# Transformer block with depthwise convolution: one band fewer on TensorE in the last image, and other offsets for the instruction order

## The chip, the cores and the metric

The kernel runs on one core of one Trainium2 chip. The core has five engines with instruction streams of their own: TensorE (PE; its weight loads are shown as PEld), VectorE (DVE), ScalarE (ACT), GpSimd (POOL) and SyncE (SP), and 16 DMA engines that they share. The metric is the device time of one execution in microseconds (us), as the median of several executions.

## What is computed

The input x is 16 images of 128 channels by 96 x 96 pixels, in fp32. For each image:

```python
x_hwc = x.transpose(0, 2, 3, 1)
xn1 = layernorm(x_hwc)                       # over the 128 channels
q, k, v = xn1 @ wq.T, xn1 @ wk.T, xn1 @ wv.T # 8 heads of 16 channels, q and k L2-normed over the pixels
attn = softmax(q @ k.T * 16 ** -0.5)         # 16 x 16 per head: channels against channels
x = x + (attn @ v) @ wp.T
xn2 = layernorm(x)
h1 = w_in @ xn2                              # 1x1 convolution, 128 -> 512 channels
h2 = depthwise_3x3(h1, w_dw)                 # 9 taps per channel, padding 1
x = x + w_out @ gelu(h2)                     # 1x1 convolution, 512 -> 128
```

## The kernel before

**Tiling.** An image is 8 bands of 12 rows; a band is 3 units of 4 rows (384 pixels). The 512 hidden channels are 4 chunks of 128. Over all images there are 128 bands, and a pair of band and chunk that goes through the vector path is a "job".

**Stages of an image.** The first norm (`norm`, line 555, with `second` false) loads x, transposes it on PE (line 614, tile pT_a), takes statistics on DVE (621), a variance and a power on POOL (628, 632), scales on ACT (668), sums the Gram matrix on PE (682) and transposes back (719). `attention` (757) makes one 128 x 128 matrix per image from the Gram matrix. The second norm begins with `x2` (564): PE multiplies the normed pixels by that matrix (571, "mix"), ACT evicts the result into one of six x buffers (580, "mixed"), and an accumulating DMA issued from POOL adds the original x to it (583, "add_x"). The transposes that follow (614, pT_b, "forth_b") read the sum; statistics, scaling and the transposes back (719, "back_b") give the padded input of the convolution.

**The feed-forward part of a band.** There are two ways for a chunk.

- The vector path, `conv_job` (886). PE makes the hidden rows (906, "hidden"), ACT copies them into a padded tile (911, "kept"). ACT multiplies two of the nine taps (919, "products"; three taps for chunk 1). The sum of these is made by accumulating DMAs issued from POOL (940), and a last one of them adds that sum to the band's tile h3. The centre tap is scaled to one, and the six (five) others are multiply-adds on DVE: the first one (924) writes h3, the rest (930) update it. ACT applies gelu (944). If the next band takes the same path, ACT first copies the last two hidden rows to the head of the padded tile (902, "halo"), and the next band makes only 12 new rows.
- By matmuls, `by_matmuls` (976), for chunk 3 alone. The 1x1 convolution and a tap are one matrix for each tap, so the nine taps are nine products per unit that add up in PSUM (990, "conv"), 27 for a band, and ACT applies gelu from PSUM (1000).

`by_pe` (1040) says which bands send chunk 3 to PE: 7 in every 15, and for the last image those that `PE_LAST` lists, counted from the end (0 is band 7, 7 is band 0). Before, these are bands 7, 6, 4, 3 and 1. With them there are 451 jobs. After the four chunks, `ffn_out` (1008) multiplies by w_out on PE (1017), DVE adds x (1024), and SP stores the band (1028), in the last band unit by unit.

**What sets the order.** Every engine runs its instructions in the order of the program, and that order is made when the program is built. Each piece of work is entered with `op` (73): its engine, an assumed duration, a place, what it reads and writes. The place is counted in jobs: the job's number plus an offset from the table `AT` that belongs to the kind of work. `Plan.order` (103) then plays the whole program through: whenever an engine is idle, it takes the piece with the lowest place among those whose inputs are done and whose buffers are free. Some buffers (`IN_TURN`, line 36) are handed out strictly by place. The starting times of this play give the program's order. The kinds whose name ends in `_0` hold for the first image.

```python
def at(kind, place, i=1):
    return place + AT[kind if i else kind + "_0"]
...
def by_pe(g):
    k = NG - 1 - g
    return k in PE_LAST if k < NB else k % PE_OF in PE_BANDS
```

Of the kernel before, what the change touches and what calls it, by code (L numbers as in the profile page):

```python
# [19 lines left out]
PE_CHUNK = 3  # L20
PE_BANDS = (0, 2, 4, 6, 8, 10, 12)
PE_OF = 15
PE_LAST = (0, 1, 3, 4, 6)
TINY = 1e-20
UNIT_MIN = 1e-18
UNIT = 4
# [8 lines left out]
X1_BUFS, XB_BUFS, PR_BUFS, H3_BUFS, ZT_BUFS = 2, 6, 5, 10, 3  # L35
IN_TURN = ("tr", "h3", "pr", "xb", "x1")
AT = dict(
    load_w=-20.2, weights=13.4, zeros=-68.05, load_a=-147.85, forth_a=-13.65, stats_a=-60.15, variance_a=574.05,
    power_a=353.05, scaled_a=35.3, gram=0.3, back_a=-44.8, place_a=177.6, attention=-146.15, mix=-16.25,
    residual=204, mixed=-47.8, add_x=-331.2, forth_b=-11.5, stats_b=-104.75, variance_b=68.55, power_b=-326.9,  # L40
    shift_b=-87.05, scaled_b=162.15, back_b=-5.95, place_b=38.15, halo=227.9, hidden=2.75, kept=-114.4,
    products=153.15, add_last=-10.05, tap=4.7, add_first=-147.85, gelu=241.95, conv=3.5, conv_gelu=5.8, out=7,
    add=-70.85, store=278.2, mix_0=-75.3, residual_0=369.55, mixed_0=-142.3, add_x_0=-398.7, gram_0=126.2,
    forth_a_0=-269.2, forth_b_0=-14.9, stats_a_0=-113.85, stats_b_0=-48.05, scaled_a_0=100.95, scaled_b_0=286.6,
    back_a_0=-115.65, back_b_0=-181.55, place_a_0=-352.8, place_b_0=-9.75, shift_b_0=-101.75, late=-3.55,
)
STEP = dict(scaled=0.3, hidden=0.1, products=0.5, tap=0.166, conv=1.6, conv_tap=0.03, out=0.8, out_part=0.05)
SLACK = 300
# [164 lines left out]
def tile_restormer_block(  # L213
# [826 lines left out]
# [4 lines that stand above are left out]
# [58 lines left out]
```

## Time and profile before

| | us |
|---|---|
| median of 3 runs | 4140.04 |
| lowest and highest of them | 4127.82, 4140.15 |
| the profiled execution, its own time | 4139.28 |
| its span, first to last instruction | 4137.5 |

| engine | busy, us | of the span |
|---|---|---|
| PE | 4064.3 | 98% |
| DVE | 4048.7 | 98% |
| ACT | 3674.7 | 89% |
| POOL | 2538.1 | 61% |

The profile is of one execution. A group of instructions is named by its line, engine and operation, with the tile written and those read: `L930 DVE ... h<-h,ratio,h` is the multiply-add at line 930. An fp32 product appears as two records of PE, so line 990 has 3,294 records for 61 bands of 27 products. PE's records overlap, since matmuls are pipelined; what one costs is read from the starts of neighbours, not from its length. `<-` after an idle time names what ended it. Granted clock is the share of its full clock that TensorE was given.

### The profile page before, as it was taken

The numbers are of one execution on the slowest core, as the hardware profiler recorded it, in microseconds if no ns is written. First come the engines' busy times: TensorE is split into PE (matmuls) and PEld (weight loads), VectorE is DVE, ScalarE is ACT, GpSimd is POOL, SyncE is SP. The second block draws the span as 40 slices with busy tenths as digits, with TensorE's granted clock in tenths as the row PEclk, the third lists the DMA queues.
The fourth block names the chain that finished last, engine by engine and source line by source line (L and its number), as shares of the span: only waits on it lengthen the run. The fifth ranks groups of instructions, "written<-read, shape, count | busy, mean of one in ns | idle before, by whom it ended". The sixth has DMA issues, their size and how long they took to land.

```text
span 4137.5 us, 52025 instructions
## 1 busy us (share of the span) xinstructions
PE 4064.3 (98%) x17217; PEld 2630.9 (64%) x17217; DVE 4048.7 (98%) x4706; ACT 3674.7 (89%) x6993; POOL 2538.1 (61%) x2357
## 2 busy tenths in 40 slices
PE   8999999999999999999999999999999999999999
PEld 6666666666666666666666666666666666666555
DVE  6999999999999999999999999999999999999998
ACT  5899989999889998999899989999889989999886
POOL 4657656566665757657566665666646666566442
PEclk9999999999999999999999999999999999999999
DMA  2999999999999999999999999999999999999998
GB/s 87 193 195 213 205 213 204 206 217 199 211 203 204 209 198 209 216 200 207 199 216 197 209 201 206 213 207 204 200 198 211 205 213 209 194 208 205 192 195 187
DMA packets 205372, 833.50 MB, mean 201 GB/s; under 512 B 23728, under 2 KB 25136, under 8 KB 205104
## 3 DMA queue, kind: packets, MB, share of 16 engines
q0 software_dynamic: 165600, 678.37, 84.6%
q1 hardware_dynamic: 38256, 151.73, 9.8%
q8 instruction: 136, 2.23, 0.2%
q14 instruction: 132, 1.08, 0.1%
q10 hardware_dynamic: 1248, 0.09, 0.0%
HBM read 148.26 MB, written 75.50 MB: 54 GB/s over the span
## 4 chain that ended last, share of the span: by engine, by line
PE 40%; DVE 10%; ACT 5%; DMA 3%; issue 2%; POOL 1%; POOLq 0%; ACTq 0%; DVEq 0%
PE h L990 11%; PE h L1017 10%; PE h L906 8%; DVE h L930 7%; PE g L682 2%; PE h L571 2%; DMA h<-pr 2%; DVE h L924 2%; PE pB_a L719 1%; ACT pr L919 1%; PE pT_b L614 1%; PE pT_a L614 1%; PE pB_b L719 1%; DMA pr<-pr 1%; ACT h L911 1%
## 5 line engine op out<-in xcount | busy, mean ns | idle before, releaser
L930 DVE SCALAR_TENSOR_TENSOR h<-h,ratio,h 128x1140 f32<-128x1140 f32 (+3 forms) x2129 | 2890.9, 1378 | 5.0
L919 ACT ACTIVATE pr<-h,ratio 128x1152 f32<-128x1152 f32 x1028 | 1337.2, 1307 | 98.7 <-DMA h<-pr 63.1
L990 PE MATMUL h<-xn,comp 128*128 128x380 f32 (+1 forms) x3294 | 1160.5, 483 | 3.6 <-ACT h L911 1.5
L1017 PE MATMUL h<-h,woutT 128*128 128x384 f32 x3072 | 1129.9, 487 | 11.4 <-ACT h L944 4.7
L906 PE MATMUL h<-xn,winT 128*128 128x384 f32 (+2 forms) x2706 | 1055.9, 494 | 8.0 <-ACT h L911 6.1
L940 POOL DMA_DIRECT2D pr<-pr x578 | 558.3, 977 | 478.3 <-ACT pr L919 312.0
L990 PEld LDWEIGHTS h<-xn,comp 128*128 128x128 f32 x3294 | 596.9, 190 | 348.8 <-issue 6.5
L911 ACT COPY h<-h 128x384 f32<-128x384 f32 (+2 forms) x1353 | 670.0, 525 | 142.0 <-PE h L906 110.8
L1017 PEld LDWEIGHTS h<-h,woutT 128*128 128x128 f32 x3072 | 555.7, 190 | 347.1 <-issue 25.0
L906 PEld LDWEIGHTS h<-xn,winT 128*128 128x128 f32 x2706 | 485.6, 190 | 302.4 <-issue 35.9
L940 POOL DMA_DIRECT2D h<-pr x450 | 447.6, 998 | 361.5 <-PE h L906 73.8
L924 DVE SCALAR_TENSOR_TENSOR h<-h,ratio 128x1152 f32<-128x1152 f32 x451 | 633.8, 1408 | 5.0 <-ACT h L911 2.8
L944 ACT ACTIVATE h<-h 128x1152 f32<-128x1152 f32 x453 | 549.4, 1216 | 14.9 <-DMA h<-pr 8.9
L632 POOL TENSOR_TENSOR rstd_a<-ve_a,mhalf 128x4 f32<-128x4 f32 x288 | 535.3, 1859 | 13.0 <-POOL ve_a L628 0.2
L628 POOL TENSOR_SCALAR ve_a<-st_a 128x4 f32<-128x4 f32 x288 | 347.3, 1206 | 286.9 <-DVE st_a L621 263.2
L632 POOL TENSOR_TENSOR rstd_b<-ve_b,mhalf 128x4 f32<-128x4 f32 x288 | 516.5, 1794 | 10.6
L672 ACT ACTIVATE zT<-pT_b,nb_b,rstd_b 128x128 f32<-128x128 f32 x1132 | 434.3, 494 | 47.4 <-DVE nb_b L636 40.6
L628 POOL TENSOR_SCALAR ve_b<-st_b 128x4 f32<-128x4 f32 x288 | 285.5, 996 | 301.9 <-DVE st_b L621 285.5
L668 ACT ACTIVATE zT<-pT_a,rstd_a 128x128 f32<-128x128 f32 x1080 | 320.3, 422 | 18.9 <-POOL rstd_a L632 17.7
L682 PEld LDWEIGHTS g<-zT 128*128 128x128 f32 x2304 | 295.1, 192 | 45.0 <-issue 4.4
L682 PE MATMUL g<-zT 128*128 128x129 f32 x2304 | 305.1, 275 | 0.0
L571 PE MATMUL h<-xn,mwT 128*128 128x384 f32 x768 | 287.1, 490 | 6.6 <-ACT h L911 3.2
(171 smaller groups left out, 3585.7 us busy)
## 6 DMA issues: line engine op xcount, KB each, us to landing
pr<-pr POOLq DMA_DIRECT2D x578, 576.0 KB, 7.5
h<-pr POOLq DMA_DIRECT2D x450, 576.0 KB, 7.7
x<-in_x_dram SPq DMA_DIRECT2D x128, 576.0 KB, 6.8
out_dram<-x SPq DMA_DIRECT2D x127, 576.0 KB, 6.3
x<-in_x_dram POOLq DMA_DIRECT2D x122, 576.0 KB, 7.2
out_dram<-x SPq DMA_DIRECT2D x3, 192.0 KB, 1.9
weights<-in_L_conv_w_in_dram SPq DMA_DIRECT2D x1, 256.0 KB, 2.9
weights<-in_L_conv_w_out_dram SPq DMA_DIRECT2D x1, 256.0 KB, 3.0
```

The lines of the kernel that those rows point to most:

```text
L628: nc.gpsimd.tensor_scalar(ve, d["mv"][:, :, 2], 1.0 / C, EPS, ALU.mult, ALU.add)
L632: nc.gpsimd.tensor_tensor(rstd, d["ve"], mhalf, ALU.pow)
L682: nc.tensor.matmul(grams[i][:, : P + 1], lhsT=zt[:, :P], rhs=zt, start=(q == 0 and k == 0), stop=(q == NU * TPU // QT - 1 and k == QT - 1),)
L906: nc.tensor.matmul(rows(ph), lhsT=winT[:, n, :], rhs=window(xn, r0 + r, e - r, 1), start=True, stop=True)
L911: nc.scalar.copy(window(h1_, r, e - r, 1), rows(d.pop(("ph", r))))
L919: nc.scalar.activation(to, shifted(t), AF.Copy, scale=ratio[:, n, t : t + 1])
L924: nc.vector.scalar_tensor_tensor(h3, shifted(t), ratio[:, n, t : t + 1], shifted(UNIT), ALU.mult, ALU.add)
L930: nc.vector.scalar_tensor_tensor(to, shifted(t)[:, lo:hi, cut], ratio[:, n, t : t + 1], to, ALU.mult, ALU.add)
L940: nc.gpsimd.dma_start(out=to, in_=d["pr", t], accum_op=ALU.add)
L944: nc.scalar.activation(h3, h3, AF.Gelu)
L990: nc.tensor.matmul(d["pc"][:, lo:hi, cut], lhsT=comp[:, t, :], rhs=window(xn, r0 + dy, UR, dx)[:, lo:hi, cut], start=(t == order[0]), stop ...
L1017: nc.tensor.matmul(rows(d["po"]), lhsT=woutT[:, n, :], rhs=h3s[g, n][:, s * UR : (s + 1) * UR, :], start=(k == 0), stop=(k == NCH - 1),)
```

## The change

`PE_LAST` loses its 4: band 3 of the last image sends chunk 3 through the vector path, and PE does chunk 3 of bands 7, 6, 4 and 1. There are 452 jobs. Nearly all offsets of `AT` get other values. No function, buffer count, assumed duration or step changes.

```diff
-PE_LAST = (0, 1, 3, 4, 6)
+PE_LAST = (0, 1, 3, 6)
...
 AT = dict(
-    load_w=-20.2, weights=13.4, zeros=-68.05, load_a=-147.85, forth_a=-13.65, stats_a=-60.15, variance_a=574.05,
-    power_a=353.05, scaled_a=35.3, gram=0.3, back_a=-44.8, place_a=177.6, attention=-146.15, mix=-16.25,
-    residual=204, mixed=-47.8, add_x=-331.2, forth_b=-11.5, stats_b=-104.75, variance_b=68.55, power_b=-326.9,
-    shift_b=-87.05, scaled_b=162.15, back_b=-5.95, place_b=38.15, halo=227.9, hidden=2.75, kept=-114.4,
-    products=153.15, add_last=-10.05, tap=4.7, add_first=-147.85, gelu=241.95, conv=3.5, conv_gelu=5.8, out=7,
-    add=-70.85, store=278.2, mix_0=-75.3, residual_0=369.55, mixed_0=-142.3, add_x_0=-398.7, gram_0=126.2,
-    forth_a_0=-269.2, forth_b_0=-14.9, stats_a_0=-113.85, stats_b_0=-48.05, scaled_a_0=100.95, scaled_b_0=286.6,
-    back_a_0=-115.65, back_b_0=-181.55, place_a_0=-352.8, place_b_0=-9.75, shift_b_0=-101.75, late=-3.55,
+    load_w=-11.35, weights=26.85, zeros=-51.2, load_a=-148.1, forth_a=-12.95, stats_a=-77.6, variance_a=582.8,
+    power_a=359.6, scaled_a=34.95, gram=0.2, back_a=-48.25, place_a=192.25, attention=-147.25, mix=-9.95,
+    residual=188.1, mixed=-47.25, add_x=-337.85, forth_b=-10.25, stats_b=-123.85, variance_b=75.75,
+    power_b=-321.2, shift_b=-86.15, scaled_b=152.35, back_b=-1.25, place_b=26, halo=237.2, hidden=2.75,
+    kept=-122.9, products=147.25, add_last=-6.5, tap=3.55, add_first=-152.4, gelu=244.25, conv=3.35,
+    conv_gelu=4.1, out=7.05, add=-83.45, store=276.95, mix_0=-81.9, residual_0=376.05, mixed_0=-142.1,
+    add_x_0=-392.4, gram_0=138.4, forth_a_0=-265.5, forth_b_0=-14.9, stats_a_0=-103.3, stats_b_0=-56.85,
+    scaled_a_0=98.55, scaled_b_0=286.35, back_a_0=-116.6, back_b_0=-170.2, place_a_0=-343.35, place_b_0=-8.15,
+    shift_b_0=-113.75, late=10.8,
 )
```

## The prediction

> **What bounds the kernel now.** I read the page's busy table first, then the chain that ended last, then the busy time by stage, and last the timeline of the final 20 us, engine by engine.
>
> The busy table and the chain of the page:
> ```profile
> span 4137.5 us, 52025 instructions
> ...
> PE 4064.3 (98%) x17217; PEld 2630.9 (64%) x17217; DVE 4048.7 (98%) x4706; ACT 3674.7 (89%) x6993; POOL 2538.1 (61%) x2357
> ...
> PE 40%; DVE 10%; ACT 5%; DMA 3%; issue 2%; POOL 1%; POOLq 0%; ACTq 0%; DVEq 0%
> ```
> PE and DVE are both within 2.2% of the span, so neither can take work without the other giving some up. Work moved from one to the other helps only if the receiver has idle time where the work lands. That is read by stage; columns are the stretch, its length, then busy us (instructions) of PE, PEld, DVE, ACT, POOL, then granted clock, DMA share and GB/s:
> ```profile
> 0.00:100.00 100.00, 84.68 (x542) 69.12 (x543) 67.89 (x198) 50.73 (x133) 40.81 (x101) 0.98 0.28 86
> 100.00:1000.00 900.00, 885.34 (x3791) 574.63 (x3790) 889.83 (x1020) 818.57 (x1570) 580.06 (x520) 1.00 0.97 205
> 1000.00:2000.00 1000.00, 989.13 (x4234) 641.69 (x4233) 989.71 (x1138) 909.31 (x1749) 648.60 (x578) 1.00 0.97 206
> 2000.00:3000.00 1000.00, 985.85 (x4186) 640.04 (x4185) 983.77 (x1125) 907.86 (x1731) 636.97 (x571) 0.99 0.97 205
> 3000.00:3800.00 800.00, 791.61 (x3365) 511.58 (x3364) 791.41 (x911) 727.61 (x1389) 507.07 (x455) 1.00 0.97 206
> 3800.00:4100.00 300.00, 293.75 (x999) 174.02 (x998) 298.93 (x293) 249.17 (x413) 120.15 (x129) 0.99 0.96 198
> ```
> DVE's idle time is 32.1 us in the first 100 us, 10.2 + 10.3 + 16.2 + 8.6 = 45.3 us from 100 to 3800, and only 1.1 us from 3800 to 4100. That last stretch is the last image, where no next image's first norm runs beside the bands. PE is idle 6.2 us there. So in the very stage that the change touches DVE is full and PE almost.
>
> The end, from the timeline (start, length, engine, line, operation, count, idle before and its releaser):
> ```profile
> 4118.28 15.64 PE L1017 MATMUL h<-h,woutT 128*128 128x384 f32 x48
> ...
> 4123.47 1.30 DVE L930 SCALAR_TENSOR_TENSOR h<-h,ratio,h 128x1045 f32<-128x1045 f32 x1
> ...
> 4124.80 2.40 ACT L944 ACTIVATE h<-h 128x384 f32<-128x384 f32 x4 [5.84 <-DVE h L930]
> ...
> 4133.96 0.56 DVE L1024 TENSOR_TENSOR x<-h,x 128x384 f32<-128x384 f32 x1 [2.02 <-PE h L1017]
> ```
> DVE's last tap ends at 4124.8, the last gelu at 4127.2, but PE still has 24 output products queued and ends at 4133.9. The chain view of the last part agrees: it lies on DVE taps from about 3797 to 4076 and on PE from 4076.7 to 4133.9, without a gap. So DVE sets the pace of the last image and PE sets its last 57 us.
>
> **The change, part 1: band 3 of the last image.** In PE_LAST the number counts from the end, so the 4 that goes is band 3. Its channel chunk 3 goes from 27 tap matmuls to the vector path (line 976 on is no longer called for it, line 886 on is).
>
> PE: an fp32 product is two records. In the timeline, 22 conv records (L990) that begin at 4084.32 are followed by the next group at 4091.37: 0.320 us each. 27 x 2 x 0.320 = 17.3 us go. Three hidden products (L906; four rows each, since band 2 hands on a halo) come: 6 x 0.323 (15.49 us over 48 in the chain's last piece) = 1.9 us. Net PE -15.4 us.
>
> DVE: six taps come, one L924 and five L930. Start to start in the last 80 us an L924 takes 1.33 us (4061.92 to 4063.25) and four L930 5.28 (4065.03 to 4070.31), so 1.33 + 5 x 1.32 = +7.9 us. The page's means (1408 and 1378 ns) hold some overlap of one instruction's end with the next one's start.
>
> ACT, by the rows of the last image: 3 x 0.504 (kept) + 2 x 1.289 (products) + 1.157 (gelu of a band) + 0.403 (band 2 now copies a halo for chunk 3) - 3 x 0.509 (gelu of a unit) = +4.1 us. ACT has 51 us idle from 3800 to 4100, so this is hidden; without that cover it would cost its 4.1.
>
> POOL issues two more accumulating DMAs, 2 x 0.93 us, in a stretch where it is busy 40%: hidden. On the queue itself: 84.6% of 4137.5 us over 1,150 transfers (578 + 450 + 122) is 3.04 us of all 16 engines each, so +6.1 us. The DMA share from 3800 to 4100 is 0.96, some 12 us free. They fit, closely. SP's stores keep their number and order.
>
> **Sum of part 1.** DVE is full, so its 7.9 us come later at the end: last tap 4124.8 + 7.9 = 4132.7. What must follow a last tap, with no PE queue in the way: 2.4 us of gelu slices, one product pair 0.65, semaphores about 0.3 (an estimate from the 0.1 to 0.3 between such steps above), the add 0.56, and the 3.0 us between that add's end (4134.5) and the span's end, for the store: 6.9 us. That gives 4139.6, **+2 us**, if the 15.4 us taken off PE empty its queue at the end. If they do not, because bands 6 and 7 are still done by PE at the very end and their buffers come free only with DVE's progress, the whole PE block slides by DVE's delay: **+8 us**. PE idles only 6.2 us in the 300 before, so its block at the end is mostly backlog and most of it should be drawn forward: I take **+4**. A gain from part 1 alone is excluded: DVE's sum grows where it has 1 us idle.
>
> One page speaks against freeing PE at all. The Trainium skill, Perfetto Trace Analysis, section Identifying the Most-Contended Engine, says that TensorE's nearness to its limit is to be read from MFU and the busy share of weight loads, not from matmul busy time; here that share is 64% of the span, and 58% from 3800 to 4100, which would make PE's relief worthless and the sum +8. The row at 4118.28, 48 records at 0.32 us with no gap, says that PE was the one waited for, and I go by the row.
>
> **Part 2: the new order.** Nearly every offset in AT changes. An offset only chooses among operations whose inputs and buffers are ready, and the work and its durations stay. Moves of a whole band or more (3.5 jobs; a job is 4137.5 / 451 = 9.2 us): mix from -16.25 to -9.95 and back_b from -5.95 to -1.25 in PE's order, place_b 38.15 to 26 in ACT's, add_last -10.05 to -6.5 on POOL, late and weights 14 jobs later at the start. No row shows the new order, so I bound it by what one and the same order shows in different stretches. DVE's idle rate from 100 to 3800 runs from 10.3 per 1000 us to 16.2. Over 3700 us the best rate gives 38 us idle, -7; the worst 60, +15. Further out: all 45.3 us of stalls gone is -45, stalls doubled +45; the first 100 us hold another 32 that the start's offsets reach. The rows lie on both sides, so I take 0 and keep both ends.
>
> Total: +4 on the profiled execution's 4139.28 (its span is 4137.5; the other 1.8 lie around it). That execution is 0.8 under the median of the three runs, 4140.04, which is nothing beside their spread of 12.3. **4143.**
>
> **Rivals.**
> *The order loses more than it did (slower).* mix is put 6.3 jobs later while forth_b, which needs its result, moves by 1.25. Between them stand the ACT eviction and POOL's accumulating load, which lands 7.2 us after issue in the median, 13.3 at worst; x buffers, six, already hold mix back, which speaks against. Today only 5 of the 122 loads keep PE's weight loads waiting, 2.5 us in all. PE runs its list in order, so behind a late forth_b stand hidden products, convs and outputs, then DVE's taps. It decides once a band loses more than 0.07 us in the mean (8.4 us over 120 bands, with the +4 past the bound below). At the worst stretch's rate it is +19 (4158), with stalls doubled +49; middle 4165.
> *The last image's DMA fills up (slower).* 6.1 us more on a queue with 12 free, where taps wait for no transfer but the gelu does. If none of the free time can be used: 7.9 + 6.1 = +14, 4153. Against it: ACT's waits on accumulating transfers in the last 337 us are 13 us in all.
> *The order gains (faster).* Half of the 45.3 us of stalls goes: -23 + 4 = -19, 4120. For it: in several 100 us stretches (300 to 400, 2300 to 2400) DVE has no idle at all, so the stalls are not inherent. Against: PE is idle 48 us in the same 3700, both would have to lose theirs together.
>
> **Chances.** What a measurement of this kernel tells from no change is about 0.3%, 12.4 us: below 4127.6 faster, above 4152.5 slower. Forecast, within it: 0.34. Order loses 0.32, DMA 0.06: slower 0.38. Order gains: 0.28. The likeliest is the forecast, 4143, with its own range 4130 to 4152. Both signs hold most of the chance between them, so the 8 in 10 reach from the gain's price, 4120, to a little past the loss's middle, 4168.
>
> **What would show it.** L990 3240 records (54 fewer), L930 2134, L924 452, L940 two more. Right: DVE idle under 3 us from 3800 to 4100, its last tap some 8 us nearer to the span's end, so fewer than 48 output records after it, PE idle in the last image up by about 15, DVE idle from 100 to 3800 between 38 and 60. Wrong: waits of pT_b on x grown from 2.5 us (first rival), gelu waiting for transfers in the last image (second), DVE idle from 100 to 3800 under 30 (third), or a first 100 us with other than about 32 idle on DVE.

## The result, and the profile after

| | before | after |
|---|---|---|
| median of 22 executions each, us | 4136.72 | 4148.07 |
| lowest and highest | 4127.82, 4144.29 | 4135.63, 4162.76 |
| the profiled execution (its span) | 4139.28 (4137.5) | 4144.05 (4142.3) |

The ratio is 1.0029, with a 95% interval of 1.0020 to 1.0038: the changed kernel is slower by 11.4 us (8 to 16), just inside the 0.3% (12.4 us) that the prediction called no change, with an interval that reaches beyond it. The two profiled executions are 4.8 us apart, and not 11.4, because the one before lies 2.6 us above its median and the one after 4.0 us below. What the two traces show has to be read with that in mind. Line numbers of the changed kernel are one higher than before from line 46 on (`AT` has one line more): 931 is the tap that was 930.

The busy table of the page after:
```profile
span 4142.3 us, 51899 instructions
...
PE 4049.7 (98%) x17169; PEld 2623.6 (63%) x17169; DVE 4056.4 (98%) x4712; ACT 3682.2 (89%) x6997; POOL 2535.3 (61%) x2359
...
L931 DVE SCALAR_TENSOR_TENSOR h<-h,ratio,h 128x1140 f32<-128x1140 f32 (+3 forms) x2134 | 2905.6, 1383 | 5.1
```
Against before, PE has lost 14.6 us of busy time and DVE has gained 7.7: the move of the work came out as counted (2,134 and 452 taps, 3,240 conv records, two more transfers).

The same stretches as before, with the same columns:
```profile
0.00:100.00 100.00, 84.71 (x531) 69.23 (x532) 67.58 (x196) 50.27 (x130) 41.53 (x102) 0.95 0.27 86
100.00:1000.00 900.00, 883.91 (x3807) 575.34 (x3807) 891.50 (x1028) 818.26 (x1577) 571.35 (x519) 1.00 0.96 204
1000.00:2000.00 1000.00, 987.67 (x4207) 639.61 (x4205) 984.58 (x1121) 908.82 (x1736) 663.84 (x575) 1.00 0.97 206
2000.00:3000.00 1000.00, 988.21 (x4207) 642.05 (x4207) 990.00 (x1132) 910.57 (x1733) 631.36 (x572) 1.00 0.97 207
3000.00:3800.00 800.00, 792.15 (x3381) 514.39 (x3379) 792.38 (x917) 732.47 (x1400) 497.48 (x458) 1.00 0.97 206
3800.00:4100.00 300.00, 275.05 (x925) 161.02 (x925) 297.86 (x293) 246.12 (x407) 123.66 (x128) 0.98 0.94 195
```
DVE's idle time from 100 to 3800 is 8.5 + 15.4 + 10.0 + 7.6 = 41.5 us (45.3 before): no sign of a worse order in this execution. From 3800 to 4100 DVE idles 2.1 us (1.1) and PE 25.0 (6.2). The freed PE time lies idle in the last image.

The end, rows of the timeline:
```profile
4131.36 2.65 DVE L931 SCALAR_TENSOR_TENSOR h<-h,ratio,h 128x1056 f32<-128x1056 f32 x2
4133.19 2.40 ACT L945 ACTIVATE h<-h 128x1152 f32<-128x1152 f32 x4 [10.23 <-DMA h<-pr]
4134.41 4.14 PE L1018 MATMUL h<-h,woutT 128*128 128x384 f32 x12 [0.36 <-ACT h L945]
...
4138.59 0.56 DVE L1025 TENSOR_TENSOR x<-h,x 128x384 f32<-128x384 f32 x1 [0.73 <-PE h L1018]
```
The last tap ends at 4134.0, 9.2 us later than before. After it PE has 12 records left, not a queue of many bands, and the span ends 8.3 us later (12.7 before).

**A mark that splits the span.** The last image can be cut off at DVE's last residual add of image 14. The busy time from that mark to the end of the last tap, and from there to the end of the span (the tail); before:
```profile
3935.70:4124.80 189.10, 187.15 (x620) 110.36 (x620) 188.68 (x176) 142.67 (x229) 66.67 (x71) 1.00 0.94 197
4124.80:4137.50 12.70, 9.12 (x29) 5.06 (x27) 2.67 (x5) 2.40 (x4) 0.00 (x0) 0.96 0.24 93
```
and after:
```profile
3931.00:4134.00 203.00, 182.13 (x586) 105.63 (x584) 198.48 (x183) 145.93 (x232) 70.16 (x73) 0.97 0.91 192
4134.00:4142.30 8.30, 4.19 (x13) 2.20 (x12) 1.69 (x4) 1.60 (x4) 0.00 (x0) 1.00 0.19 71
```
From the mark on, 201.8 us became 211.3: +9.5. DVE's busy time up to the last tap grew by 9.8 (7.9 of taps; 0.9 are two residual adds that now come ahead of the last tap; the rest is a tap at the mark), its idle time by 4.1 (0.4 to 4.5), and the tail shrank by 4.4. The longest of DVE's waits there is one that the trace before does not have. By the view of waits (us in total, times, longest):
```profile
DVE h L925 <- PE h L1018: 3.1, 1, 3.1
```

### The profile page after: what moved, and what is told of

Read it like the earlier page. It is cut to its first block, busy times and chain, and to the rows that moved or that the text cites. A ratio compares the mean times of both kernels' runs of the same rounds, so it can differ in the third digit from the quotient of the medians.

```text
span 4142.3 us, 51899 instructions
## 1 busy us (share of the span) xinstructions
PE 4049.7 (98%) x17169; PEld 2623.6 (63%) x17169; DVE 4056.4 (98%) x4712; ACT 3682.2 (89%) x6997; POOL 2535.3 (61%) x2359
## 4 chain that ended last, share of the span: by engine, by line
PE 41%; DVE 36%; ACT 9%; DMA 7%; issue 3%; POOL 3%; POOLq 0%; ACTq 0%; DVEq 0%
DVE h L931 25%; PE h L1018 10%; PE h L991 10%; PE h L907 8%; DVE h L925 5%; DMA h<-pr 3%; DMA pr<-pr 3%; ACT pr L920 3%; PE g L683 3%; PE h L572 2%; DVE st_a L622 2%; DVE x L1025 2%; DVE st_b L622 2%; PE pB_a L720 1%; ACT zT L673 1%
## 5 line engine op out<-in xcount | busy, mean ns | idle before, releaser
L991 PE MATMUL h<-xn,comp 128*128 128x380 f32 (+2 forms) x3240 | 1130.9, 482 | 2.4 <-ACT h L912 1.7
L941 POOL DMA_DIRECT2D pr<-pr x579 | 569.6, 994 | 458.4 <-ACT pr L920 288.1
L633 POOL TENSOR_TENSOR rstd_a<-ve_a,mhalf 128x4 f32<-128x4 f32 x288 | 519.7, 1805 | 12.2 <-POOL ve_a L629 0.2
L633 POOL TENSOR_TENSOR rstd_b<-ve_b,mhalf 128x4 f32<-128x4 f32 x288 | 507.4, 1763 | 11.3
```

Of the source, the lines that this page charges most:

```text
L633: nc.gpsimd.tensor_tensor(rstd, d["ve"], mhalf, ALU.pow)
L941: nc.gpsimd.dma_start(out=to, in_=d["pr", t], accum_op=ALU.add)
L991: nc.tensor.matmul(d["pc"][:, lo:hi, cut], lhsT=comp[:, t, :], rhs=window(xn, r0 + dy, UR, dx)[:, lo:hi, cut], start=(t == order[0]), stop ...
```

## The experiments

After the result three theories stood side by side. Theory 1: the moved band costs some 5 us, as the two traces show, and the new order costs the other 6 in the mean. Theory 2: the order costs all of it. Theory 3: the moved band does. Runs that were sent together ran on one chip, with the kernel before run between them; ratios are to that.

| kernel | order of images 0 to 14 | bands of the last image on PE | ratio to before, 95% interval | mark to last tap + tail, us |
|---|---|---|---|---|
| before_again | before's | 7 6 4 3 1 | 0.9996, 0.9986 to 1.0007 | 189.1 + 12.7 |
| old_order_4 | another | 7 6 4 1 | 1.0036, 1.0023 to 1.0049 | 198.5 + 13.6 |
| old_order_6 | another | 7 6 5 4 3 1 | 1.0086, 1.0074 to 1.0098 | 205.0 + 13.6 |
| drift_old_5 | another | 7 6 4 3 1 | 1.0009, 0.9999 to 1.0019 | 189.7 + 12.7 |
| pin_old_4 | before's | 7 6 4 1 | 1.0014, 1.0006 to 1.0023 | 198.3 + 12.7 |
| pin_old_drop6 | before's | 7 4 3 1 | 1.0024, 1.0014 to 1.0033 | 197.3 + 10.2 |
| pin_old_drop7 | before's | 6 4 3 1 | 1.0037, 1.0023 to 1.0050 | 197.1 + 14.5 |
| after_again | after's | 7 6 4 1 | 1.0022, 1.0013 to 1.0031 | 203.0 + 8.3 |
| after_c | after's | 7 6 4 1 | 1.0039, 1.0026 to 1.0051 | 202.5 + 8.4 |
| new_order_5 | another | 7 6 4 3 1 | 1.0052, 1.0038 to 1.0066 | 204.4 + 8.1 |
| pin_new_5 | after's | 7 6 4 3 1 | 1.0041, 1.0025 to 1.0057 | 202.5 + 8.1 |
| pin_new_5_b | after's | 7 6 4 3 1 | 1.0054, 1.0041 to 1.0066 | 202.4 + 8.1 |

The last column is from each kernel's trace. For the same program it repeats within 0.5 us from execution to execution (before 201.8 twice; after 211.3, 211.3 and 210.9), while the whole time spreads over 16 to 27 us. So it is the sharp instrument here, and the ratio the blunt one.

**The two halves, taken apart plainly.** The old offsets with four bands:

```diff
-PE_LAST = (0, 1, 3, 4, 6)
+PE_LAST = (0, 1, 3, 6)
```

> The kernel before with PE_LAST = (0, 1, 3, 6) alone: band 3 moves to the vector path, all offsets stay. Theory 1 (part 1 costs what DVE's extra taps leave after PE's shorter queue, about +5; the new order costs the other 6): 4141 to 4142, ratio 1.001, last tap 8 to 9 us later, fewer than 48 output records after it. Theory 2 (the order costs all 11): 4136 to 4138, ratio 1.000. Theory 3 (the moved band costs all 11, since the model's old offsets suited it no better): 4147 to 4149, ratio 1.003.

The new offsets with five:

```diff
-PE_LAST = (0, 1, 3, 6)
+PE_LAST = (0, 1, 3, 4, 6)
```

> The changed kernel with PE_LAST = (0, 1, 3, 4, 6) as before: the new offsets alone. Theory 1: 4142 to 4144, ratio 1.0016. Theory 2: 4147 to 4149, ratio 1.003. Theory 3: 4136 to 4138, ratio 1.000. In theories 1 and 2 its executions also spread as wide as the changed kernel's (some 27 us over 22 executions, against 16 before).

The changed kernel again, on the same chip:

> The changed kernel once more, for its time on the same chip as the other three, and for a second trace. All theories: ratio 1.002 to 1.004. If the order's cost is a stall that comes and goes, this trace shows DVE idle from 100 to 3800 at another place or of another size than the first one's 41.5 us.

Measured: 1.0036, 1.0052, and 1.0022 for both halves together. All three theories fail at once: by the medians each half alone costs more than the whole (the intervals of old_order_4 and of the whole overlap), so they do not add up. What makes the comparison unfit is the instruction order. In the trace of old_order_4, PE's order leaves that of before at 296 us and DVE's at 299, over 3600 us ahead of the band that was moved. The places of norms and attentions are `g * band`, with `band = len(jobs) / NG`; one job more makes every band 1/128 job longer, and with it the whole program is planned anew. A constant that names one band had changed 15 images. The split had to be made otherwise.

**Six bands on PE**, the opposite direction, planned anew in the same way:

```diff
-PE_LAST = (0, 1, 3, 4, 6)
+PE_LAST = (0, 1, 2, 3, 4, 6)
```

> The kernel before with PE_LAST = (0, 1, 2, 3, 4, 6): band 5 as well goes to PE, the change in the opposite direction. If PE sets the end (its queue of 15 us after the last tap), PE's 15.4 us more come out at the end nearly whole: 4149 to 4153, ratio 1.003 to 1.004, DVE idle in the last image 8 us or more. If DVE alone sets it, 8 us less: 4128 to 4130, ratio 0.998.

Measured: 1.0086, more than either theory gave. In the last image it is 218.6 us, 16.8 over before, about PE's 15.4: DVE idles 21.8 us from the mark to its last tap. So PE's load counts too, and five bands lie between two sides that both cost. The other 18 us of the median lie outside the last image, with an order that is a different one; where, the trace taken does not show, since DVE idles 45.1 us from 100 us to the mark in it and 46.2 in before's.

**The same cut with the order pinned.** With the band length held, the order stays before's up to 3960 us:

```diff
-PE_LAST = (0, 1, 3, 4, 6)
+PE_LAST = (0, 1, 3, 6)
...
-    band = len(jobs) / NG
+    band = 451 / NG
```

> PE_LAST = (0, 1, 3, 6) with the offsets of before, and the length of a band, by which all norms and attentions are placed, held at 451 / 128 jobs. The program's order is then that of before up to about 3960 us, and only the moved band and what follows it differ: part 1 by itself. Theory A (part 1 costs DVE's 7.9 us less what PE's shorter queue gives back; the 18 us of the unpinned kernel came from 15 images in another order): +2 to +8, ratio 1.0005 to 1.002, PE idle 15 us more from 3800 on, tail after the last tap 8 us in place of 12.7. Theory B (the moved band itself costs what the unpinned kernel showed): +15 to +20, ratio 1.0036 or more.

The length alone, with no work moved (`band = 452 / NG`, five bands on PE):

> The kernel before with one change: the length of a band is held at 452 / 128 jobs in place of 451 / 128. No work moves and PE_LAST stays; the places of norms and attentions drift against the jobs by up to 0.9 job at the end, as they do in any kernel whose PE_LAST has one band fewer. Theory A: the order is another one from about 300 us on, and that alone costs 8 to 18 us: ratio 1.002 to 1.0045. Theory B: nothing, ratio within 0.999 to 1.001.

No change at all:

> The kernel before, unchanged: what the comparison shows for no change at all, and a second trace of it. All theories: ratio within 0.999 to 1.001.

Part 1 alone is slower by 0.14% (0.06 to 0.23), 5.8 us, and its trace has 9.2 us in the last image; Theory A's size by the ratio, over its upper end of 8 by the trace. The tail of 8 us that it expected did not come: it is 12.7, as before. Theory A's other half missed: the drift alone measures 0.09%, with an interval that touches none, and not the 8 to 18 us expected. Drift and band together, 0.23%, do not reach the 0.36% of the unpinned kernel, though the intervals overlap. before_again shows that a comparison of like with like comes out at nothing.

Where pin_old_4's 9.2 us are, the same two stretches of its trace:
```profile
3931.50:4129.80 198.30, 179.32 (x571) 103.33 (x572) 196.40 (x182) 146.44 (x232) 68.05 (x73) 0.96 0.93 193
4129.80:4142.50 12.70, 9.13 (x29) 5.07 (x27) 2.73 (x6) 2.40 (x4) 0.00 (x0) 1.00 0.24 93
```
DVE's busy time is up by 7.7, its idle time by 1.5 (0.4 to 1.9), and the tail is 12.7 as before. PE idles 19.0 us in the first stretch, where it idled 2.0. Most of that goes into two waits for ACT's copy of hidden rows (line 911):
```profile
PE h L1017 <- ACT h L911: 6.7, 2, 6.4
PE h L571 <- ACT h L911: 5.8, 1, 5.8
```
The first row of PE's last block, from the timelines, before:
```profile
4076.66 6.04 PE L990 MATMUL h<-xn,comp 128*128 128x384 f32 x18
```
and in pin_old_4, with the block's last row:
```profile
4080.41 6.04 PE L990 MATMUL h<-xn,comp 128*128 128x384 f32 x18 [1.49 <-DVE x L1024]
...
4123.29 15.64 PE L1017 MATMUL h<-h,woutT 128*128 128x384 f32 x48
```
The block begins 148.9 us after the mark, when a residual add of DVE frees its PSUM bank; before it began at 4076.7, 141.0 after the mark, its weight load released by a residual add as well, after a wait of 0.77 us. It slid by 7.9, DVE's delay, and kept its 48 records at the end. None of the PE time that band 3 gave up was drawn forward.

**Where the relief falls.** Band 6 or band 7 in place of band 3, pinned to the old order: `PE_LAST = (0, 3, 4, 6)` and `PE_LAST = (1, 3, 4, 6)`.

> Old offsets, band length held at 451 / 128, PE_LAST = (0, 3, 4, 6): band 6 goes to the vector path in place of band 3. The order is that of before until late in the last image. From the end of image 14 (its last residual add) to the span's end before takes 201.8 us, the pinned kernel without band 3 211.0. Theory P (it matters where PE is relieved: band 6's tap products stand in PE's last 57 us, band 3's long before): DVE +7.9, tail after the last tap 12.7 down to 8, so 203 to 206, ratio 1.000 to 1.001. Theory Q (a band costs 9 us wherever it is, since PE's outputs wait for DVE anyway): 210 to 212, ratio 1.0014.

> The same with PE_LAST = (1, 3, 4, 6): the very last band goes to the vector path. Its chunk 3 is then the last job and its product comes first in each output sum, so all 12 output products of the band wait for the last gelu. Theory P: PE is relieved at the end, but the tail has 24 records in place of the least possible, so DVE +7.9 and a tail of 12 to 15 us: 208 to 213 from the end of image 14, ratio 1.001 to 1.002. Theory Q: 210 to 212 as well, so this run speaks only together with the one before: P wants this one 4 us or more above it, Q the same.

In the last image band 6 costs 5.7 us and band 7 9.8, against band 3's 9.2. Theory P's order is right, its size for band 6 is not (207.5 from the mark to the end, for 203 to 206): the tail went to 10.2, not 8. Theory Q's 210 to 212 fails for band 6. In band 6's trace a gelu holds PE for 2.48 us ahead of its last 12 records, and DVE's last add ends 7.2 us after the last tap. Band 7 leaves 24 records after the last tap, as expected. The ratios, 1.0024 and 1.0037, are higher than the last image alone would make (1.0014 and 1.0024); the intervals reach down to these.

**The new order with five bands, pinned.**

```diff
-PE_LAST = (0, 1, 3, 6)
+PE_LAST = (0, 1, 3, 4, 6)
...
-    band = len(jobs) / NG
+    band = 452 / NG
```

> The changed kernel with PE_LAST = (0, 1, 3, 4, 6), the length of a band held at its 452 / 128: the new order of the first 15 images, and the last image as before in its split. Theory A: part 2 by itself, what the change costs less part 1's few us, ratio 1.000 to 1.002. If part 1 costs nothing, the change's own 1.0022 to 1.0029. If the new order suits only four bands, PE's queue at the end comes back and it is over 1.004, as unpinned.

> The new order with five bands on PE once more (band length 452 / 128), beside the changed kernel on the same chip. Its first 15 images are instruction for instruction those of the changed kernel, and in the traces its last image took 210.6 us against 211.3. Theory A: within 0.1% of the changed kernel beside it, and the 0.41% of the first run came from stalls that vary from chip to chip and run to run. Theory C (the new order suits four bands only): 0.15% or more above it again.

> The changed kernel on the same chip. All theories: ratio 1.002 to 1.003; from the end of image 14 to the span's end 211.3 us as in both traces so far; the rest of its cost, 0 to 2 us, in the 15 images before. Where POOL's small norm operations last over 4 us, DVE idles next to them; a chip with many such ones shows the longer time.

Twice this kernel was slower than Theory A allowed: 0.41%, for 0.29% at most, and 0.54% against after_c's 0.39% on the same chip. The 0.17% between these two medians lie on Theory C's side, but the intervals overlap. after_c itself lies over the 0.2 to 0.3% expected of it. The traces say more, and speak against Theory C: PE's queue did not come back at the end (12 records after the last tap), and the last image is no longer than the changed kernel's. That of pin_new_5:
```profile
3952.30:4154.80 202.50, 193.31 (x636) 113.23 (x634) 191.05 (x178) 144.46 (x228) 66.88 (x71) 1.00 0.89 187
4154.80:4162.90 8.10, 4.19 (x13) 2.20 (x12) 1.69 (x4) 1.58 (x4) 0.00 (x0) 1.00 0.19 73
```
Its last image takes 210.6 us, within a microsecond of the changed kernel's 211.3, with another split. DVE has 7.4 us less to do and idles 11.4 us in place of 4.5. Its longest waits there, by the view of waits:
```profile
DVE h L925 <- PE h L1018: 4.3, 1, 4.3
DVE st_b L622 <- PE pT_b L615: 3.4, 1, 3.4
DVE x L1025 <- PE h L1018: 1.5, 1, 1.5
```
In this order DVE waits for PE, so PE's band costs it as much as its own taps do. Under the new offsets the moved band is about free (211.3 - 210.6); under the old ones it costs 9.2. And the new offsets alone cost 8.8 in the last image with the old split. That is the same 9 us paid either way, and once: the old order with five bands kept DVE busy but for 0.4 us, and each of the two changes by itself leaves that point. Why the two costs are so near in size is not shown.

What the first 15 images add: from 100 us to the mark, DVE idles 46.2, 39.6, 43.0, 44.7 and 45.5 us in the five executions with before's order (before, before_again, pin_old_4, pin_old_drop6, pin_old_drop7), 43.8 in the mean. There are five with after's order too, since pin_new_5 and pin_new_5_b keep the changed kernel's order up to 3969 us: 42.3, 38.0, 51.8, 61.4 and 56.9 us (after, after_again, after_c, pin_new_5, pin_new_5_b), 50.1 in the mean. On the two chips that ran both orders, 39.6 and 43.0 stand against 61.4, and 44.7 and 45.5 against 51.8 and 56.9. So the excess of pin_new_5 over the changed kernel lies where the two programs are the same, and not in the last image. Whether the new order costs some 6 us there or only scatters more stays open: one program gave 38.0 and 51.8. It is room enough for the part of the measured 11.4 us that lies beyond the last image's 9.5; 8 to 16 less 9.5 leaves -1 to +6 for it.

## Why the prediction was right, and where its sizes were off

**The forecast** was no clear change, 4143, from a cost of 4. It came out at 4148.07, 11.4 us over the median of before: the same side, within the range of 4130 to 4152, and near that range's upper end. The call of no clear change held by 1 us, and that is luck in part. Each half of the change costs about 9 us in the last image, the sum had 4 and 0 for them, and the total stayed under 12.4 because the two do not add up, which the prediction did not say. The 4 were also counted from 4139.28, 2.6 us over the median of 22, which brings 4143 nearer to the result than +4 is to +11.4.

**What bounds the kernel** held: DVE is the pace of the last image. Its idle time from 3800 to 4100 stayed under 3 us, and the extra taps came out one for one (7.7 us busy in pin_old_4, for 7.9 counted).

**The sum of part 1** was mis-sized: "most of it should be drawn forward: I take +4". It was 9.2, with the old order and nothing else changed, over the +8 of its other case, in which "the whole PE block slides by DVE's delay". That case is the one that came. PE's block at the end was not backlog that could start at any time. Its first product waits for a PSUM bank that a residual add of DVE frees, and it slid with DVE by 7.9 us; DVE's own waits for PE added 1.5. That PE was busy up to 98% ahead of the block says that there was no room, and not that the block would move into room once it was made. The queue behind the last tap was also read too long: of the 48 records that begin at 4118.28, 27 (13 to 14 products, not 24) begin after that tap, so "fewer than 48" was true of the kernel before and told nothing.

**The tail** was counted as 6.9 us at least. In the changed kernel, which did empty PE's queue, it is 8.3, 4.4 less than before and not "some 8": 12 records in place of 2 begin after the last tap. The 4.4 us gained there were lost again, since DVE idles 4.1 us more before the last tap, 3.1 of them in one wait for an output product (line 925 behind line 1018).

**The rule on weight loads** as a measure of TensorE, which the prediction cites from the Trainium skill, Perfetto Trace Analysis, section Identifying the Most-Contended Engine, would have made PE's relief worthless and the sum +8. With the old order the sum was 9.2, for another reason than too much room on PE: old_order_6, with one more band on PE, lost 16.8 us in the last image, which an engine with 42% of headroom would hardly have done. Its order is another one, but PE is busy there for 202.2 of the 205.0 us from the mark to the last tap. The row decides; PE was full.

**The new order** was taken as 0, with -7 and +15 from rows. In images 0 to 14 the traces leave it between nothing and some 6 us (idle times of 38.0 to 61.4 us, against 39.6 to 46.2), inside those bounds. The list of larger moves left out DVE's own: stats_a, stats_b and add go 17, 19 and 13 jobs forward. In the last image it is not 0: 8.8 us with the old split, and nothing on top of the moved band. The prediction treated the two parts as terms of a sum, and they are not.

**The rivals.** The first one's sign, waits of the transposes for the x load, grew from 3.1 to 4.5 us in all over PE and its weight loads: not it. The second one's sign did show: gelu waited for transfers in the last image. ACT's rows for the gelu from 3800 us on, before and after:
```profile
L944 ACT ACTIVATE h<-h 128x1152 f32<-128x1152 f32 (+1 forms) x44 | 50.6, 1157 | 8.7 <-DVE h L930 5.8 <-DMA h<-pr 2.9
L945 ACT ACTIVATE h<-h 128x1152 f32<-128x1152 f32 (+1 forms) x46 | 52.9, 1159 | 13.6 <-DMA h<-pr 13.6
```
But the DMA share up to the last tap fell from 0.94 to 0.91, so the queue did not fill up, and PE waited only 0.36 us for the gelu behind the longest of these waits (10.2 us, at 4133.19). The two more transfers are not it either: pin_old_4 has them and costs the same 9 us, with 7.7 us of such waits of ACT from the mark to the last tap, where before has 6.2. The third did not happen; DVE's idle time did not halve in any trace.

## What to carry to other kernels

Work taken off an engine that is full helps only if what stands behind it may start earlier. Look at what releases the first instruction of the block at the end: a buffer freed by the other full engine ties the block to that engine. With an order that a planner makes, a constant for one band can replan the whole program; hold the planner's other inputs still before the times of two versions are compared, and cut the span at a mark that repeats to half a microsecond when the whole does not.

## What the runs showed of the hardware

Executions of one instruction order differ by stalls of some microseconds at single places. Some of them begin with one small POOL instruction of the norm. In pin_new_5, on POOL and on DVE, rows of the timeline:
```profile
1863.30 10.13 POOL L629 TENSOR_SCALAR ve_a<-st_a 128x4 f32<-128x4 f32 x1 [1.72 <-DVE st_a L622]
```
```profile
1863.12 1.29 DVE L931 SCALAR_TENSOR_TENSOR h<-h,ratio,h 128x1045 f32<-128x1045 f32 x1
1864.33 1.41 DVE L925 SCALAR_TENSOR_TENSOR h<-h,ratio 128x1152 f32<-128x1152 f32 x1
1865.66 5.16 DVE L931 SCALAR_TENSOR_TENSOR h<-h,ratio,h 128x1056 f32<-128x1056 f32 x4
1870.74 1.41 DVE L925 SCALAR_TENSOR_TENSOR h<-h,ratio 128x1152 f32<-128x1152 f32 x1
1872.07 1.30 DVE L931 SCALAR_TENSOR_TENSOR h<-h,ratio,h 128x1045 f32<-128x1045 f32 x1
1873.29 0.55 DVE L1025 TENSOR_TENSOR x<-h,x 128x384 f32<-128x384 f32 x1
```
An operation on 4 elements a partition takes 10.1 us, under an unbroken row of DVE taps, and ends as the first instruction begins that is not a tap. PE then waits 4.9 us in one piece, by the view of waits of that stretch, and DVE 3.3 us for PE:
```profile
ACT zT L669 <- POOL rstd_a L633: 5.1, 1, 5.1
PE pB_a L720 <- ACT zT L669: 4.9, 1, 4.9
DVE st_b L622 <- PE pT_b L615: 3.3, 1, 3.3
```
In the changed kernel the same instruction of the same program order took 1.17 us, at the boundary of two taps:
```profile
1859.03 1.17 POOL L629 TENSOR_SCALAR ve_a<-st_a 128x4 f32<-128x4 f32 x1 [1.72 <-DVE st_a L622]
```
Over pin_new_5 this instruction's durations run from 0.19 us over a median of 1.27 to 10.1. The Trainium skill, SBUF — State Buffer, section Who interferes with whom, says that a DVE instruction with two SBUF inputs contends with a GpSimd instruction that reads SBUF, and the taps at lines 925 and 931 have two. The rows agree, and add that POOL may miss the boundary between taps and then wait through eight of them. No run here took the taps or the POOL operations away, so that this is the cause of the spread between executions is argued and not shown: the changed kernel's three profiled executions had 9, 1 and 7 small POOL operations over 4 us after the first 100 us and took 4144.1, 4141.2 and 4153.4 us, an order that does not follow the counts alone; the two of pin_new_5 and pin_new_5_b had 10 and 7 and took 4165.0 and 4158.6 us.
